# A graph layer on one core: placing matrices built per chunk, additions set ahead of column copies, and 17 more blocks of rows copied instead of gathered

## The chip, the cores and the metric

The kernel runs on one core of a Trainium2 chip. The metric is the device time of one launch in microseconds (us), the median of several runs. The engines of the core are TensorE (PE, matrix products), VectorE (DVE), ScalarE (ACT), GpSimd (POOL) and SyncE (SP); each runs its own instructions in order.

## The reference

A graph of 12,500 nodes (128 numbers each) has 412,500 edges, sorted by destination. Every edge takes the features of its source node, weighs them by a small network of its own eight scalars and by its four attributes, and the results are summed at the destination. The output is a layer norm of the input plus a mix.

```python
f0 = x0 @ W1_0e / sqrt(32); f1 = einsum('nui,uw->nwi', x1, W1_1o) / sqrt(32)   # features of nodes
e0, e1 = feat0[edge_src], feat1[edge_src]                  # gathered for every edge
h = gelu(gelu(edge_scalar_attr @ W_mlp1 / sqrt(8)) @ W_mlp2 / 8)
w00, w01, w10, w11 = h @ Wp_00, h @ Wp_01, h @ Wp_10, h @ Wp_11
out0_a = w00 * e0 * ea0;  out0_b = w11 * sum(e1 * ea1, -1) / sqrt(3)
out1_a = (w01 * e0) * ea1;  out1_b = w10 * e1 * ea0
n0, n1 = segment_sum(concat(out*_a, out*_b), edge_dst) / sqrt(32) / sqrt(2)
y = c * self(x) + s * (n0 @ W2_0e, n1 @ W2_1o) / 8
out = layernorm(x + y)
```

## The kernel before

Edges are worked on in **runs** of 512 (four blocks of 128 edges, one edge per partition), 806 in all; four runs make a **chunk** (CH = 4), 202 in all. The loop goes over runs `s`, with `c, k = divmod(s, CH)`, so k is a run's place in its chunk. The order of instructions on PE, ACT, DVE and SP is the order in which this loop writes them; nothing moves them.

**Rows for the edges.** A table of features (one row of 128 numbers per node) lies in HBM. `gather(s)` issues one indirect DMA on POOL for each block of 128 edges of run s (L197), 19 runs ahead of its use, into one of 20 buffers G. Some blocks come another way:

- The *picked* blocks: the transposed input xT lies in SBUF, one column per node. `pick_nodes` loads up to 32 column addresses into registers of an engine by one register load (L154, TENSOR_LOAD), and `pick` then copies that many columns, one instruction each, into a tile gt (L165 on DVE, L167 on ACT). After 128 columns, `picked_rows` multiplies gt by the weights on PE (L173) and ACT writes the block into G (L174). `COLS` says over how many runs 128 columns are spread: 5 on DVE (24 or 28 columns in each run) and 6 on ACT. DVE picks one block in 5 runs, ACT one in 6.
- One block of every 14th run comes by 128 row DMAs from SP (`aid`).
- The first 18 runs gather raw input rows, and PE makes the features.

**One run on DVE.** `messages(s)` makes three products of weights and G (L574, then L577 twice). `placing(s)` compares a row of numbers with one column to make a 0/1 matrix PL (L600). Then come the register load (L154) and the column copies of the run (L165).

**One chunk.** PE sums the messages of a run into windows (`segments`, L591), and at k = 1 of the next chunk `place(c - 1)` multiplies by PL (L607). At k = 2 `add(c - 1)` loads four addresses (L611) and adds four results into the running sums (L616); each addition waits for the one before it. At k = 3 `select(c + 1)` builds the 0/1 matrices of the next chunk by three operations (L559, L566, L567, of which L566 waits for L559). About every eighth chunk, `norm` (L636 to L668) finishes 512 nodes at k = 3, and `clear_sums` (L371) clears the next tile of sums in four pieces. The order at the end of a run is this:

```python
messages(s); placing(s); pick_nodes(DVE, s); pick(DVE, P)
if k == 2: add(c - 1)
if k == 3: norm(...)
elif clearing: clear_sums(...)
if k == 3: select(c + 1)
```

Of the kernel before, what the change touches and what calls it, by code (L numbers as in the profile page):

```python
# [8 lines left out]
F32 = mybir.dt.float32  # L9
# [3 lines left out]
OP = mybir.AluOpType  # L13
PE = mybir.EngineType.PE
ACT = mybir.EngineType.Activation
DVE = mybir.EngineType.DVE
# [4 lines left out]
P = 128  # L21
# [4 lines left out]
SB = P * Q  # L26
J = 8
W = 32
CH = 4
# [13 lines left out]
AID_FROM = 36  # L43
AID_LEAD = 16
STEPS = 12
COLS = {DVE: 5, ACT: 6}
COL_Q = {DVE: Q - 2, ACT: Q - 3}
COL_TURN = {DVE: (8, 0), ACT: (16, 1)}
LNB = 2
# [3 lines left out]
def gnn_kernel(ctx: ExitStack, tc: tile.TileContext, x, src, dst, ea4, ea8, w1_0, w1_1, wm1, wm2,  # L53
# [8 lines left out]
    nc = tc.nc  # L62
# [43 lines left out]

    picked = {}
    for e, per in COLS.items():
        picked[e], (t, k) = [], COL_TURN[e]
        while True:  # L110
            at = t + per + 1
            at += (k - at) % CH
            if at + 2 >= NS - 1:
                break
            picked[e].append((t, at, at + 2))
            t += per
    pick_of = {(e, s): i for e, g in picked.items() for i, (_, _, s) in enumerate(g)}
    assert AID_FROM >= raw_runs and AID_LEAD < LEAD and P % ROWS == 0 and STEPS <= AID
    assert all(raw_runs <= g[0][2] and 0 < len(g) <= 2 * P for g in picked.values())
# [5 lines left out]
    def aid_load():  # L125


        nc.sync.dma_start(aid_at, sub(src, AID_FROM * SB + (Q - 1) * P, [[AID * SB, len(aided)], [1, P]]))
        nc.vector.tensor_scalar(aid_at, aid_at, float(4 * P), None, op0=OP.mult)
        for e, g in picked.items():  # L130
            cycle = CH // math.gcd(CH, COLS[e])
            for h in range(0, len(g), P):
                part = g[h:h + P]
                rows = cst.tile([len(part), P], I32, name=f"pick{len(pick_rows)}")
                for i in range(min(cycle, len(part))):
                    n = len(part[i::cycle])
                    nc.sync.dma_start(rows[i::cycle], sub(src, part[i][2] * SB + COL_Q[e] * P,
                                                          [[cycle * COLS[e] * SB, n], [1, P]]))
                nc.vector.tensor_scalar(rows, rows, 4.0, float(x_at), op0=OP.mult, op1=OP.add)
                for i in range(len(part)):  # L140
                    pick_rows[e, h + i] = rows[i:i + 1]
# [2 lines left out]

    def pick_nodes(e, s):

        per = COLS[e]
        i, t = divmod(s - COL_TURN[e][0], per)
        if not 0 <= i < len(picked[e]):
            return  # L150
        if t == 0:
            GT[e, i] = wk.tile([P, P], F32, name=f"gt{list(picked).index(e)}", bufs=3)
        r0, r1 = (n * (P // 4) // per * 4 for n in (t, t + 1))
        _, r = nc.values_load_multi_w_load_instructions(  # L154
            pick_rows[e, i][:, r0:r1], engines=[e], min_val=x_at, max_val=x_at + 4 * (N - 1),
            skip_runtime_bounds_check_because="addresses of columns")
        for k in range(r1 - r0):
            at = r[k].with_bounds(guaranteed_mod_val=0, out_of_modulus=4)
            picking[e].append((GT[e, i][:, r0 + k:r0 + k + 1], x_bytes[:, bass.ds(at, 4)].bitcast(F32)))
# [433 lines left out]
        if r % 2 or s == NS - 1:  # L593
            nc.scalar.activation(SG[c][:, r // 2 * 2:r + 1, :], SEG[c][:, r // 2 * 2:r + 1, :], AF.Copy)  # L594

    def placing(s):

        b, r = divmod(s, P)
        PL[s] = wk.tile([P, P], F32, name="pl", bufs=CH + 1)
        nc.vector.tensor_scalar(PL[s], iota, colv[b][:, r:r + 1], None, op0=OP.is_equal)  # L600

    def place(c):
        ns = min(CH, NS - c * CH)
        ST[c] = pt = ps.tile([P, CH, 4, W], F32, name="m", bufs=1)
        for k in range(ns):
            s = c * CH + k
            nc.tensor.matmul(pt[:, k].rearrange("p a n -> p (a n)"), SG[c][:, k, :], PL[s], start=True, stop=True)  # L607

    def add(c):
        ns = min(CH, NS - c * CH)  # L610
# [189 lines left out]
    with tc.manual_schedule(engines={PE, ACT, DVE, SP}):  # L800
        load_raw_rows(nc.sync, 0, min(2, raw_runs))
        load_w1(nc.scalar)
        if raw_runs > 2:
            load_raw_rows(nc.scalar, 2, raw_runs)
        for s in range(min(LEAD - 2, raw_runs)):
            gather(s)
        nc.vector.tensor_scalar(ident, diag, 0.0, None, op0=OP.is_equal)
        for b in range(min(3, NG)):
            XT[b] = load_nodes(b)
        make_wf()  # L810
        clear()
        loads = list(weight_loads())
        extra = {2: lambda: load_edges(0), 3: lambda: load_attributes(0), NG // 2 - 2: lambda: turn_attributes(0), 4: lambda: load_raws(0), NG // 2: lambda: load_indices(0),
                 NG // 2 + 3: make_w1b, NG // 2 + 5: make_ws, NG - 6: lambda: radial(0), NG - 4: lambda: mlp1(0),
                 NG - 2: lambda: mlp2(0), NG - 1: make_wpost}
        for b in range(NG + 2):
            if b < NG:
                turn(b)
            if 0 < b <= NG:
                features_of(b - 1)  # L820
            if 1 < b:
                store_nodes(nc.scalar, table, b - 2, PF[b - 2])
            if b + 3 < NG:
                XT[b + 3] = load_nodes(b + 3)
            if b > 4 and loads:
                nc.sync.dma_start(*loads.pop(0))
            if b in extra:
                extra[b]()
        assert not loads
        for c in range(1, min(EDGES_AHEAD, NCH)):  # L830
            load_edges(c)
        if aided:
            aid_load()
        for s in range(min(LEAD - 2, raw_runs), min(LEAD - 1, NS)):
            gather(s)
        if NCH > 1:
            radial(1)
            mlp1(1)
            mlp2(1)
        weights(0)  # L840
        select(0)
        turn_rows(0)
        features(0)
        find_first()
        new_sums()
        nc.vector.memset(A["next"], 0.0)
        A["now"] = A["next"]
        new_sums()
        clearing = [(0, a) for a in range(4)]
        pick_nodes(ACT, 0)  # L850
        for s in range(NCH * CH + CH):
            c, k = divmod(s, CH)
            if s + LEAD - 1 < NS:
                gather(s + LEAD - 1)
            if k == 3 and c + EDGES_AHEAD < NCH:
                load_edges(c + EDGES_AHEAD)
            if s % P == P // 2 - 16 and (s // P + 1) * P < NS:
                load_raws(s // P + 1)
            if s % P == P // 2 and (s // P + 1) * P < NS:
                load_indices(s // P + 1)  # L860
            if s % ET == 8 and s - 8 + ET < NS:
                load_attributes(s // ET + 1)
            for t in range(P // ROWS):
                a = s + AID_LEAD - t * STEPS // (P // ROWS)
                if a in aided:
                    aid(a, t)
            end = c == NCH - 1
            if k % 2 == 0:
                pick(ACT, len(picking[ACT]) // 2)
            if k % 2 == 0 and s + 2 < NS:  # L870
                weights(s + 2)
            if 0 < s <= NS:
                segments(s - 1)
            if k == 0 and c + 2 < NCH:
                radial(c + 2)
            if k == (0 if end else 1) and 0 < c <= NCH:
                place(c - 1)
            if s % ET == 21 and s - 21 + ET < NS:
                turn_attributes(s // ET + 1)
            for e in picked:  # L880
                if (e, s + 2) in pick_of:
                    picked_rows(e, pick_of[e, s + 2])
            if k > 1 and c + 2 < NCH:
                pick(ACT, P)
                (mlp1 if k == 2 else mlp2)(c + 2)
                if k == 3 and c + 3 == NCH:
                    nc.scalar.activation(spent, ones, AF.Sqrt)
            pick(ACT, P)
            pick_nodes(ACT, s + 1)
            if s + 1 < raw_runs:  # L890
                turn_rows(s + 1)
            if s < NS:
                messages(s)
                placing(s)
                pick_nodes(DVE, s)
                pick(DVE, P)
            if s + 1 < raw_runs:
                features(s + 1)
            if k == (1 if end else 2) and 0 < c <= NCH:
                add(c - 1)  # L900
            if k == (1 if end else 3) and 0 < c <= NCH:
                norm(due.get(c - 1, []), last=c == NCH)
                clearing += [(c, a) for a in range(4)] if c - 1 in due and c < NCH else []
            elif clearing:
                clear_sums(clearing.pop(0)[1])
            if k == 3 and c + 1 < NCH:
                select(c + 1)
            if s == NS - 8:
                count_odd()

# [30 lines left out]
```

## Time and profile before

| | |
|---|---|
| median of 3 runs | 3655.97 us (3654.6 to 3658.94) |
| profiled execution | 3654.6 us, span of its instructions 3652.8 us |
| busy: PE, DVE, ACT, POOL | 72%, 84%, 65%, 75% |
| gathers on POOL | 2880 (72 of them from the raw input) |
| column copies on DVE, on ACT | 20,224 and 16,640 |
| register loads for them on DVE | 790 |

The profile lists groups of instructions by line, with busy time, the mean duration of one and the idle time of the engine just before them. A duration runs from the start to the end of an instruction; on DVE and ACT the next one starts before that end, so what an instruction costs in a row of work is the distance between starts. Register loads run on the engine's sequencer, which hands out the engine's instructions; the profile does not count them as busy, and marks them with a q (DVEq).

### The profile page before, as it was taken

To read this page: it belongs to the slowest core of one execution; us is meant where nothing else is said; L and a number is where in the kernel's file an instruction comes from. 1 tells how busy PE (TensorE), PEld (TensorE's weight loads), DVE (VectorE), ACT (ScalarE), POOL (GpSimd) and SP (SyncE) were. 2 spreads that over 40 slices of the span, in tenths; PEclk is the share of its full clock that TensorE was granted. 3 is DMA by queue.
4 is the path that set the end of the run, shared out by engine and by line. 5 is a ranking of instruction groups with operands and counts; after the bars stand their busy time and mean duration, and the time that the engine had idled before them with its cause. 6 is when DMAs were issued, how large, how long until landed. Compare 5 with 4: busy or idle time off the path is not lost.

```text
span 3652.8 us, 129429 instructions
## 1 busy us (share of the span) xinstructions
PE 2618.5 (72%) x29857; PEld 1938.9 (53%) x29857; DVE 3077.8 (84%) x25457; ACT 2391.7 (65%) x18614; POOL 2736.6 (75%) x2887
## 2 busy tenths in 40 slices
PE   5777777877677777677777677677677677677676
PEld 5555555655455555455555455555455555455554
DVE  3688898898898888887887888888888798798886
ACT  2377677677677667666766667666666676676673
POOL 7767777777777777777777777777777777777775
PEclk8989898788888878887788787887887787788877
DMA  9222332333332333322323322223222233233222
GB/s 207 57 57 67 63 63 64 63 63 71 63 63 65 63 63 70 63 62 63 63 59 68 67 60 63 67 60 69 64 62 63 63 63 63 65 63 62 59 64 48
DMA packets 578767, 243.66 MB, mean 67 GB/s; under 512 B 482186, under 2 KB 527072, under 8 KB 577984
## 3 DMA queue, kind: packets, MB, share of 16 engines
q0 software_dynamic: 92160, 188.93, 20.4%
q1 hardware_dynamic: 464542, 39.90, 8.9%
q10 hardware_dynamic: 21282, 6.47, 0.8%
q8 instruction: 238, 3.90, 0.5%
q14 instruction: 545, 4.46, 0.4%
HBM read 222.26 MB, written 12.80 MB: 64 GB/s over the span
## 4 chain that ended last, share of the span: by engine, by line
DVE 31%; issue 16%; POOL 16%; PE 10%; DMA 9%; SPq 7%; ACT 7%; DVEq 4%; ACTq 0%; POOLq 0%
POOL G L197 16%; DVE gt L165 13%; DMA G<-table,idx 8%; DVE M L577 7%; SPq L184 5%; ACT gt L167 3%; DVEq L154 3%; DVE M L574 3%; DVE acc L616 2%; DVE pl L600 2%; PE h L636 2%; PE seg L591 2%; PE w L532 2%; SPq L180 2%; DVE S L567 1%
## 5 line engine op out<-in xcount | busy, mean ns | idle before, releaser
L197 POOL DMA_INDIRECT G<-table,idx x2808 | 2667.1, 950 | 867.8 <-issue 737.2
L167 ACT ACTIVATE gt<-xT 128x1 f32 x16640 | 1664.4, 191 | 146.5 <-issue 144.9
L165 DVE COPY gt<-xT 128x1 f32 x20224 | 1301.6, 145 | 205.0 <-issue 194.2
L532 PE MATMUL w<-wpb,h 64*128 64x128 f32 x6448 | 730.9, 332 | 336.3 <-DVE M L577 334.0
L591 PE MATMUL seg<-M,S 128*32 128x128 f32 x12896 | 652.0, 322 | 419.1 <-DVE M L577 278.5
L532 PEld LDWEIGHTS w<-wpb,h 64*128 64x128 f32 x6448 | 587.5, 226 | 503.9 <-DVE M L577 388.9
L577 DVE TENSOR_TENSOR M<-w,G 128x384 f32<-128x384 f32 x1576 | 797.5, 548 | 0.0
L591 PEld LDWEIGHTS seg<-M,S 128*32 128x32 f32 x12896 | 343.6, 123 | 607.6 <-issue 152.1
L594 ACT ACTIVATE sg<-seg 128x256 f32<-128x256 f32 x403 | 150.9, 374 | 404.0 <-PE seg L591 391.5
L574 DVE TENSOR_TENSOR M<-w,G 128x256 f32<-128x256 f32 x788 | 323.4, 410 | 107.9 <-DMA G<-table,idx 93.7
L515 PE MATMUL h<-h,w2b 64*64 64x256 f32 x3232 | 319.2, 413 | 90.2 <-ACT h L504 87.4
L607 PE MATMUL m<-pl,sg 128*128 128x128 f32 x1612 | 333.0, 370 | 1.5 <-DVE acc L616 0.8
L607 PEld LDWEIGHTS m<-pl,sg 128*128 128x128 f32 x1612 | 282.1, 264 | 59.7 <-issue 57.6
L174 ACT ACTIVATE G<-h 128x128 f32<-128x128 f32 x288 | 79.3, 275 | 331.0 <-PE h L173 293.7
L500 PE MATMUL h<-eT,w1b 64*128 64x128 f32 x3232 | 280.3, 322 | 5.8 <-ACT eT L493 5.8
L500 PEld LDWEIGHTS h<-eT,w1b 64*128 64x128 f32 x3232 | 237.8, 222 | 56.1 <-issue 45.5
L515 PEld LDWEIGHTS h<-h,w2b 64*64 64x64 f32 x3232 | 146.6, 139 | 216.9 <-ACT h L504 177.4
L616 DVE TENSOR_TENSOR acc<-m,acc 128x128 f32 x806 | 234.2, 291 | 30.8 <-issue 2.7
L600 DVE TENSOR_SCALAR pl<-iota,colv 128x128 f32<-128x128 f32 x806 | 241.2, 299 | 5.1 <-PE m L607 5.1
L504 ACT ACTIVATE h<-h 128x512 f32<-128x512 f32 x404 | 215.7, 585 | 35.3 <-PE h L500 33.8
L520 ACT ACTIVATE h<-h 128x512 f32<-128x512 f32 x404 | 214.1, 580 | 19.8 <-PE h L515 14.0
L173 PE MATMUL h<-wf,gt 128*128 128x128 f32 x576 | 146.0, 345 | 14.4 <-ACT eT L493 10.2
(117 smaller groups left out, 1489.8 us busy)
## 6 DMA issues: line engine op xcount, KB each, us to landing
G<-table SPq DMA_DIRECT2D x7040, 0.5 KB
G<-table,idx POOLq DMA_INDIRECT x2808
e<-in_edge_attr SPq DMA_DIRECT2D x201, 64.0 KB
xt<-in_x SPq DMA_DIRECT2D x24, 256.0 KB
table<-ft ACTq DMA_DIRECT2D x24, 256.0 KB
xt<-in_edge_attr SPq DMA_DIRECT2D x24, 256.0 KB
out<-y SPq DMA_DIRECT2D x24, 256.0 KB
xt<-in_dst SPq DMA_DIRECT2D x5, 256.0 KB
```

The costliest lines, as they stand in the source:

```text
L165: nc.vector.tensor_copy(to, col)
L167: nc.scalar.activation(to, col, AF.Copy)
L197: nc.gpsimd.indirect_dma_start(out=G[s][:, q, :], out_offset=None, in_=x if s < raw_runs else table, in_offset=bass.IndirectOffsetOnAxis(a ...
L500: nc.tensor.matmul(p1[h][:, j // 2, j % 2, :], w1b[rows, j, :], eT[c][rows, :], start=True, stop=True)
L515: nc.tensor.matmul(p2[r][k * HID:(k + 1) * HID, h * n:(h + 1) * n], w2b[rows, :], H1[c][h][rows, k * n:(k + 1) * n], start=True, stop=True)
L532: nc.tensor.matmul(WP[i][:, q, :], H2[c][q % 2][rows, k, q // 2, :], wpb[rows, :], start=True, stop=True)
L574: nc.vector.tensor_tensor(m[:, :, :, :MUL], w[:, :, :2 * MUL].rearrange("p q (a u) -> p q a u", a=2), g[:, :, None, :MUL].to_broadcast([P, ...
L577: nc.vector.tensor_tensor(m[:, :, j, MUL:].rearrange("p q (i u) -> p q i u", i=3), w[:, :, None, (2 + j) * MUL:(3 + j) * MUL].to_broadcast ...
L591: nc.tensor.matmul(SEG[c][q * W:(q + 1) * W, r, :], own[:, r * Q + q, col:col + W], M[s][:, q, h, :], start=h == 0, stop=h == 1)
L600: nc.vector.tensor_scalar(PL[s], iota, colv[b][:, r:r + 1], None, op0=OP.is_equal)
L607: nc.tensor.matmul(pt[:, k].rearrange("p a n -> p (a n)"), SG[c][:, k, :], PL[s], start=True, stop=True)
L616: nc.vector.tensor_tensor(a, ST[c][:, k], a, op=OP.add)
```

## The change

Three things change.

- Picks on DVE are spread over 4.5 runs instead of 5: blocks of 4 and of 5 runs take turns, with 32 columns in each run of the first kind and 24 or 28 of the second. There are 175 picked blocks in place of 158, and 2863 gathers in place of 2880.
- `placing` is called once a chunk, at k = 0, and makes the four matrices by one operation on 128 x 512, with two buffers in place of five small ones.
- The register load and the column copies of a run come last in the run: behind the additions, the norm and the selection. Clearing is done at k = 1 alone.

```diff
-COLS = {DVE: 5, ACT: 6}
+COLS = {DVE: 4.5, ACT: 6}
...
-            at = t + per + 1
+            t, z = (t0 + int(n * per) for n in (len(picked[e]), len(picked[e]) + 1))
+            at = z + 1
             at += (k - at) % CH
...
-            picked[e].append((t, at, at + 2))
-            t += per
+            picked[e].append((range(t, z), at, at + 2))
...
-            cycle = CH // math.gcd(CH, COLS[e])
+            cycle = next(n for n in range(1, P) if n * COLS[e] % CH == 0)
...
-    def placing(s):
-        b, r = divmod(s, P)
-        PL[s] = wk.tile([P, P], F32, name="pl", bufs=CH + 1)
-        nc.vector.tensor_scalar(PL[s], iota, colv[b][:, r:r + 1], None, op0=OP.is_equal)
+    def placing(c):
+        n = min(CH, NS - c * CH)
+        b, r = divmod(c * CH, P)
+        PL[c] = wk.tile([P, CH, P], F32, name="pl")
+        nc.vector.tensor_tensor(PL[c][:, :n], iota[:, None, :].to_broadcast([P, n, P]),
+                                colv[b][:, r:r + n, None].to_broadcast([P, n, P]), op=OP.is_equal)
...
                 messages(s)
-                placing(s)
-                pick_nodes(DVE, s)
-                pick(DVE, P)
+                if k == 0:
+                    placing(c)
...
             if k == (1 if end else 2) and 0 < c <= NCH:
                 add(c - 1)
             if k == (1 if end else 3) and 0 < c <= NCH:
                 norm(due.get(c - 1, []), last=c == NCH)
...
-            elif clearing:
+            elif k == 1 and clearing:
                 clear_sums(clearing.pop(0)[1])
             if k == 3 and c + 1 < NCH:
                 select(c + 1)
+            if s < NS:
+                pick_nodes(DVE, s)
+                pick(DVE, P)
```

More of the change, by code (lines that the diff above doesn't have):

```diff
@@ L108, in gnn_kernel @@
     for e, per in COLS.items():
-        picked[e], (t, k) = [], COL_TURN[e]
+        picked[e], (t0, k) = [], COL_TURN[e]
         while True:
-            at = t + per + 1
+            t, z = (t0 + int(n * per) for n in (len(picked[e]), len(picked[e]) + 1))
+            at = z + 1
             at += (k - at) % CH
@@ L114, in gnn_kernel @@
                 break
-            picked[e].append((t, at, at + 2))
-            t += per
+            picked[e].append((range(t, z), at, at + 2))
+    step_of = {(e, s): (i, s - g[i][0][0]) for e, g in picked.items() for i in range(len(g)) for s in g[i][0]}
     pick_of = {(e, s): i for e, g in picked.items() for i, (_, _, s) in enumerate(g)}
@@ L137, in aid_load @@
                     nc.sync.dma_start(rows[i::cycle], sub(src, part[i][2] * SB + COL_Q[e] * P,
-                                                          [[cycle * COLS[e] * SB, n], [1, P]]))
+                                                          [[int(cycle * COLS[e]) * SB, n], [1, P]]))
                 nc.vector.tensor_scalar(rows, rows, 4.0, float(x_at), op0=OP.mult, op1=OP.add)
@@ L145, in pick_nodes @@
     def pick_nodes(e, s):
-        per = COLS[e]
-        i, t = divmod(s - COL_TURN[e][0], per)
-        if not 0 <= i < len(picked[e]):
+        if (e, s) not in step_of:
             return
+        i, t = step_of[e, s]
+        per = len(picked[e][i][0])
         if t == 0:
@@ L606, in place @@
             s = c * CH + k
-            nc.tensor.matmul(pt[:, k].rearrange("p a n -> p (a n)"), SG[c][:, k, :], PL[s], start=True, stop=True)
+            nc.tensor.matmul(pt[:, k].rearrange("p a n -> p (a n)"), SG[c][:, k, :], PL[c][:, k, :], start=True, stop=True)
     def add(c):
```

## The prediction

> **What bounds the kernel now.** I read the page first, for POOL's gathers and DVE's copies and placing matrices.
>
> ```profile
> span 3652.8 us, 129429 instructions
> L197 POOL DMA_INDIRECT G<-table,idx x2808 | 2667.1, 950 | 867.8 <-issue 737.2
> L165 DVE COPY gt<-xT 128x1 f32 x20224 | 1301.6, 145 | 205.0 <-issue 194.2
> L600 DVE TENSOR_SCALAR pl<-iota,colv 128x128 f32<-128x128 f32 x806 | 241.2, 299 | 5.1 <-PE m L607 5.1
> ```
>
> POOL's gaps are "issue", 0.3 us behind each gather: gathers follow each other every 1.25 us without a stop. DVE has 194.2 us of "issue" ahead of copies. Which of the two engines sets the end? I located the messages of each run (L574). Run 20 starts at 205.2 us, run 40 at 280.6, run 260 at 1202.1, run 796 at 3593.1. Next, DVE's waits in two stretches: runs 40 to 260, then run 260 to 3610.0 us.
>
> ```profile
> DVE gt L165 <- issue: 38.0, 89, 1.7
> DVE bst L645 <- ACT y L641: 24.7, 6, 5.0
> ...
> DVE gt L165 <- issue: 149.9, 324, 1.7
> DVE M L574 <- DMA G<-table,idx: 84.3, 68, 3.0
> DVE bst L645 <- ACT y L641: 50.9, 16, 6.0
> ```
>
> In the first stretch no message waits for a gather: POOL is ahead, DVE goes at its own rate, (1202.1 - 280.6) / 55 = 16.75 us a chunk. In the second, messages wait for gathers: 2407.9 / 135 = 17.84 us a chunk, POOL's rate. So DVE has about 1.1 us a chunk to spare. The question is whether the change costs DVE more than that.
>
> The decisive row is the register load. DVE's timeline in one stretch, with the chain of waits through it:
>
> ```profile
> 1015.46 0.28 DVE L600 TENSOR_SCALAR pl<-iota,colv 128x128 f32<-128x128 f32 x1
> 1015.65 1.54 DVE L165 COPY gt<-xT 128x1 f32 x24
> 1018.56 1.54 DVE L165 COPY gt<-xT 128x1 f32 x24
> 1020.02 1.26 DVE L616 TENSOR_TENSOR acc<-m,acc 128x128 f32 x4
> 1021.20 0.41 DVE L574 TENSOR_TENSOR M<-w,G 128x256 f32<-128x256 f32 x1
> 1022.46 0.28 DVE L600 TENSOR_SCALAR pl<-iota,colv 128x128 f32<-128x128 f32 x1
> 1023.25 0.15 DVE L165 COPY gt<-xT 128x1 f32 x1 [0.52 <-issue]
> ...
> 1020.99 0.04 DVE acc L616
> 1021.02 0.05 issue
> 1021.07 0.05 DVEq L574
> ```
>
> The loads' own rows, two single ones:
>
> ```profile
> L154 DVEq TENSOR_LOAD <-pick x1: 1612/1612/1612, 1016.8 to 1016.8; - x1
> L154 DVEq TENSOR_LOAD <-pick x1: 1858/1858/1858, 1021.3 to 1021.3; - x1
> ```
>
> The first (24 columns) starts at 1016.8, before the copies of the previous run are done: the sequencer runs ahead, and messages and placing hide the load. The second (28) stands behind additions. Each addition waits for the one before; only when the fourth has started (1020.99) does the sequencer go on, and the load starts at 1021.30. It ends at 1023.16, the copies start 0.09 later, and DVE has stood idle 0.52 us even though three messages and a placing lay between.
>
> **The change, part by part (us a chunk, DVE at its own rate, from 16.75).**
>
> *Stalls before, removed:* 38.0 / 55 = 0.69.
>
> *Length of the new loads.* 24 columns take about 1.64 us and 28 about 1.90 over the whole trace (1.61 and 1.86 in the rows above), 0.064 per column; 32 columns then take 2.16 (estimate). By the loop, 261 loads have 24, 174 have 28 and 352 have 32: 1.93 on average. Copies start 0.09 behind.
>
> *k = 2.* The load now stands directly behind the additions. It starts 0.01 after the fourth, which takes 0.21 to the next start. Idle: 1.93 + 0.09 + 0.01 - 0.21 = 1.82.
>
> *k = 3.* The load stands behind the selection. L566 waits for L559, so the load starts with L566; L566 and L567 cover 0.21 + 0.47 (from start to start) = 0.68. Idle: 1.93 + 0.09 + 0.02 - 0.68 = 1.36.
>
> *k = 1.* Only three messages, 0.33 + 2 x 0.46 = 1.26, lie ahead of the load, and a clearing (0.40) in about half of the chunks. Loads in clear stretches start some 0.35 ahead of the messages. 1.93 + 0.09 - 0.35 - 1.26 = 0.41, without clearing; with it nearly nothing. Loads at k = 1 stalled 0.14 more than this reasoning gives, so I take 0.35, between 0.1 and 0.6.
>
> *k = 0.* Messages and the large placing cover 1.86: 0.08, at most 0.3.
>
> Together 3.61, so 2.92 more than before.
>
> *Copies.* 17 blocks x 128 = 2176 more, 11.4 a chunk. From start to start (1.54 - 0.145) / 23 = 0.061: +0.69.
>
> *Placing.* Four by 0.19 (1015.46 to 1015.65) are 0.76, with 0.03 of waits 0.79. The trace has no comparison of 128 x 512. The nearest rows are L566 (128 elements, 0.21) and L567 (384, 0.47): 0.13 per 128, so 0.60. Bounds 0.47 and 0.79. Taken: -0.19. [...]
>
> *Norm.* About every eighth chunk, DVE waits some 4 us for ACT (24.7 / 6). The copies of k = 2 and their stall now lie between the additions and that wait, which shortens it by about 1.4: -0.18 (0 to -0.35). PE and ACT keep their places.
>
> *Gathers.* 17 fewer x 1.25 = 21 us less on POOL, 17.73 a chunk; worth that only if POOL is still last. The 17 more products on PE and evictions on ACT (0.3 us each) lie beside other work.
>
> *Start.* Eight more loads of column addresses on SP, some 0.65 each, lie ahead of the loop, whose first messages start at 107.8: 0 to 5 us. In the raw runs DVE waits for ACT anyway. I take +2, at most +9.
>
> The sum is 16.75 + 2.92 + 0.69 - 0.19 - 0.18 = 19.99, above POOL's 17.73: DVE becomes the bound from the start, and POOL will run 20 buffers ahead. Behind each stalled load stand the copies, then the next run's messages, for which PE's sums and POOL's free buffers wait.
>
> Total: 205.2 + 2 up to run 20; 776 runs = 194 chunks x 19.99 = 3878; from run 796 to the end 59.7 before, about 50 now, since no gather holds the last runs back: 4135 for the span. The profiled execution was 1.8 above its span and 1.4 below the median: **4137 us**, slower by 13%. The terms' bounds are worth about ±0.4 a chunk: 4055 to 4215.
>
> **Rivals.**
>
> *A, gathers still set the pace (faster).* The sequencer gets past instructions that wait, and the loads start under messages as now. Then DVE needs 16.75 + 0.69 - 0.19 = 17.25, POOL's 17.73 rules, and the time is 3656 - 21 = 3635. It decides if new stalls stay under 17.73 - 17.25 = 0.48 a chunk. For it: loads with nothing waiting ahead of them start early. Against it: the second load above, and the register operations ahead of the additions, which the trace has only some 0.01 after the start of the preceding addition. [...]
>
> *B, half of it.* Only the load behind the additions is exposed; behind the selection it starts early, and 1.36 becomes about 0.3. 18.93 x 194 + 257 + 3 = 3932. Against it: L566 waits for L559 as an addition waits for its predecessor.
>
> *C, more.* Emptied by the stalls, the sequencer loses its lead at k = 0 and k = 1 as well, and loads start 0.1 after the messages, as behind additions now: about 0.45 more at each, 0.9 a chunk, 4310. For it: late in the run some loads do start so. Against it: 24 or more copies of 0.061 give the sequencer time to catch up.
>
> **How the numbers follow.** Forecast 0.77, A 0.04, B 0.07, C 0.12. A range from 4010 to 4230 takes in the forecast's own bounds and reaches toward B and C; A, most of B and half of C lie outside. No change means within 0.2% (7 us), about what a measurement of this kernel can tell. Faster comes from A alone, 0.04; same 0.01, where stalls just reach the break-even; slower 0.95.
>
> **What would show it.** "Issue" ahead of the copies should rise from 194 us to about 700, mostly in pieces of about 1.8 us behind the additions and 1.4 us behind the selection; DVE's busy time should rise by about 100 us, its share fall; messages should no longer wait for gathers; POOL should wait for messages. Loads starting ahead of the additions or the selection would prove me wrong, as would a chunk under 18 us.

## The result, and the profile after

The changed kernel takes 4111.97 us (median of 4 runs, 4103.59 to 4114.89) beside 3655.28 us for the kernel before (4 runs): a ratio of 1.1247, 95% interval 1.1224 to 1.127. The profiled execution took 4103.59 us, its span 4101.8 us.

The page of the changed kernel: span, engines, and the groups of gathers, column copies and the first message of a run (busy, mean ns | idle before, and what ended it):

```profile
span 4101.8 us, 131172 instructions
PE 2854.1 (70%) x29891; PEld 2112.8 (52%) x29891; DVE 3148.9 (77%) x27026; ACT 2412.9 (59%) x18631; POOL 2752.2 (67%) x2870
L198 POOL DMA_INDIRECT G<-table,idx x2791 | 2681.8, 961 | 1233.6 <-issue 781.2
L166 DVE COPY gt<-xT 128x1 f32 x22400 | 1430.9, 144 | 666.8 <-issue 655.7
L575 DVE TENSOR_TENSOR M<-w,G 128x256 f32<-128x256 f32 x788 | 326.7, 415 | 0.6 <-ACT G L175 0.2
```

The first message of a run in the kernel before, and POOL's waits for messages before and now (us in total, times, longest):

```profile
L574 DVE TENSOR_TENSOR M<-w,G 128x256 f32<-128x256 f32 x788 | 323.4, 410 | 107.9 <-DMA G<-table,idx 93.7
```

```profile
POOL G L197 <- DVE M L577: 37.9, 123, 0.7
POOL G L198 <- DVE M L578: 353.0, 163, 14.1
```

The bound has moved. Idle time ahead of the copies rose from 205 to 667 us, nearly all of it "issue". Messages waited 108 us before, mostly for gathers, and now 0.6. POOL, which had paused 868 us in its own steps of 0.3, now pauses 1234, 353 of them for messages. Every engine's busy share fell, DVE's from 84% to 77%: the engine that sets the end is less busy than before, because it stands idle between its own instructions.

VectorE's timeline through one chunk, k = 2 and 3, then 0 and 1 of the next:

```profile
2023.56 1.26 DVE L619 TENSOR_TENSOR acc<-m,acc 128x128 f32 x4
2027.01 2.03 DVE L166 COPY gt<-xT 128x1 f32 x32 [2.19 <-issue]
...
2030.74 0.55 DVE L568 TENSOR_TENSOR S<-oh,e 128x384 f32<-128x384 f32 x1
2032.80 2.27 DVE L166 COPY gt<-xT 128x1 f32 x32 [1.50 <-issue]
...
2036.24 0.68 DVE L602 TENSOR_TENSOR pl<-iota,colv 128x512 f32<-128x512 f32 x1
2036.94 2.03 DVE L166 COPY gt<-xT 128x1 f32 x32
...
2040.29 0.48 DVE L372 MEMSET acc<- 128x512 f32 x1
2040.97 2.04 DVE L166 COPY gt<-xT 128x1 f32 x32 [0.20 <-issue]
```

Idle time stands above all where the load follows a waiting instruction: 2.19 us behind the additions, 1.50 behind the selection, none behind the large placing, 0.20 behind a clearing. The chain of waits through the first of these places (start, length, what):

```profile
2024.53 0.29 DVE acc L619
2024.82 2.10 DVEq L155
2026.92 0.09 issue
2027.01 1.46 DVE gt L166 x22
```

The row of the load at this place (duration min/median/max in ns, then when it starts):

```profile
L155 DVEq TENSOR_LOAD <-pick x1: 2382/2382/2382, 2024.5 to 2024.5; - x1
```

The load starts at 2024.5, with the fourth addition, and the chain runs through it: 2.10 us in which DVE has nothing to do. Copies start 0.09 after its end. It is the same at every such place from run 40 to 790: the 187 loads at k = 2 start a median 0.014 us after the fourth addition, the 187 at k = 3 a median 0.016 us after L567, the operation of the selection that waits for L560, and none starts before it.

### The profile page after: what moved, and what is told of

It is laid out like the page before. It is cut to its first block, busy times and chain, and to the rows that moved or that the text cites. A ratio compares the mean times of both kernels' runs of the same rounds, so it can differ in the third digit from the quotient of the medians.

```text
span 4101.8 us, 131172 instructions
## 1 busy us (share of the span) xinstructions
PE 2854.1 (70%) x29891; PEld 2112.8 (52%) x29891; DVE 3148.9 (77%) x27026; ACT 2412.9 (59%) x18631; POOL 2752.2 (67%) x2870
## 3 DMA queue, kind: packets, MB, share of 16 engines
q0 software_dynamic: 91616, 187.81, 17.9%
## 4 chain that ended last, share of the span: by engine, by line
DVE 29%; issue 6%; SPq 6%; DVEq 5%; PE 4%; ACT 2%; DMA 1%; POOL 1%; ACTq 0%; POOLq 0%
DVE gt L166 14%; DVE M L578 7%; DVEq L155 5%; SPq L185 5%; DVE M L575 2%; DVE acc L619 2%; PE h L639 1%; SPq L181 1%; DVE pl L602 1%; ACT gt L168 1%; POOL G L198 1%; DVE S L567 1%; DMA G<-table,idx 1%; PE seg L592 0%; DVE acc L372 0%
## 5 line engine op out<-in xcount | busy, mean ns | idle before, releaser
L166 DVE COPY gt<-xT 128x1 f32 x22400 | 1430.9, 144 | 666.8 <-issue 655.7
L533 PE MATMUL w<-wpb,h 64*128 64x128 f32 x6448 | 831.0, 360 | 466.2 <-DVE M L578 462.7
L592 PE MATMUL seg<-M,S 128*32 128x128 f32 x12896 | 691.6, 342 | 499.7 <-DVE M L578 385.6
L533 PEld LDWEIGHTS w<-wpb,h 64*128 64x128 f32 x6448 | 666.2, 249 | 653.0 <-DVE M L578 530.1
L592 PEld LDWEIGHTS seg<-M,S 128*32 128x32 f32 x12896 | 363.7, 129 | 700.1 <-issue 295.5
L516 PE MATMUL h<-h,w2b 64*64 64x256 f32 x3232 | 333.7, 421 | 93.9 <-ACT h L505 91.2
L610 PE MATMUL m<-pl,sg 128*128 128x128 f32 x1612 | 374.7, 405 | 1.3 <-ACT sg L595 1.3
L610 PEld LDWEIGHTS m<-pl,sg 128*128 128x128 f32 x1612 | 319.0, 294 | 68.9 <-issue 67.0
L516 PEld LDWEIGHTS h<-h,w2b 64*64 64x64 f32 x3232 | 148.4, 140 | 229.1 <-ACT h L505 192.5
L619 DVE TENSOR_TENSOR acc<-m,acc 128x128 f32 x806 | 233.6, 290 | 23.6 <-PE m L610 2.1
L174 PE MATMUL h<-wf,gt 128*128 128x128 f32 x610 | 171.7, 378 | 7.6 <-DVE bst L648 7.6
L174 PEld LDWEIGHTS h<-wf,gt 128*128 128x128 f32 x610 | 155.8, 310 | 10.8 <-issue 10.8
```

The costliest lines, as they stand in the source:

```text
L166: nc.vector.tensor_copy(to, col)
L174: nc.tensor.matmul(pt, GT.pop((e, i)), wf, start=True, stop=True)
L516: nc.tensor.matmul(p2[r][k * HID:(k + 1) * HID, h * n:(h + 1) * n], w2b[rows, :], H1[c][h][rows, k * n:(k + 1) * n], start=True, stop=True)
L533: nc.tensor.matmul(WP[i][:, q, :], H2[c][q % 2][rows, k, q // 2, :], wpb[rows, :], start=True, stop=True)
L592: nc.tensor.matmul(SEG[c][q * W:(q + 1) * W, r, :], own[:, r * Q + q, col:col + W], M[s][:, q, h, :], start=h == 0, stop=h == 1)
L619: nc.vector.tensor_tensor(a, ST[c][:, k], a, op=OP.add)
```

## Experiments

Two theories were set against each other. Theory 1: the register load lost the work that covered it, because the sequencer doesn't get past an instruction that waits. Theory 2: the place or the number of the copies, not the load, costs the time.

Of twelve runs, eight fell on two other chips, on which the kernel before itself takes 5681 and 5585 us. Four are told first, from chips where it takes about 3655 us.

**All but the order** (e6): the changed kernel with load and copies put back behind the messages.

```diff
                 messages(s)
                 if k == 0:
                     placing(c)
+                pick_nodes(DVE, s)
+                pick(DVE, P)
...
-            elif k == 1 and clearing:
+            elif clearing:
...
-            if s < NS:
-                pick_nodes(DVE, s)
-                pick(DVE, P)
```

> The changed kernel with the order of before: load and copies directly behind the messages and the placing. Theory 1: loads of 1.93 us stand behind messages alone in three runs of four; idle 0.05 at k = 0, 0.6 at k = 1, 0.46 at k = 2, 0.72 at k = 3; 18.3 us a chunk, about 3820 us. The order's share of the change is then some 290 us, the rest comes from the longer loads, the lost cover and the copies. Theory 2 (order free): 4112 us.

Measured: 3713.03 us, ratio to the kernel before 1.0155 (1.014 to 1.0171). So putting the order back takes 4112 - 3713 = 399 of the 457 us away, and theory 2's "order free" falls. (What the order would cost the kernel before by itself was forecast at 300 us; e1 and e1b tried it, both on the other two chips.) From the page:

```profile
L166 DVE COPY gt<-xT 128x1 f32 x22400 | 1433.5, 144 | 301.4 <-issue 292.2
L575 DVE TENSOR_TENSOR M<-w,G 128x256 f32<-128x256 f32 x788 | 320.7, 407 | 0.8 <-issue 0.4
```

As many copies, 301 us of idle time ahead of them in place of 667, and still no message that waits for a gather: DVE remains the bound. On average (runs 40 to 790) the idle time ahead of a run's copies was, by k, 0.04, 0.31, 0.36 and 0.78 us, in place of 0.08, 0.20, 1.82 and 1.27 in the changed kernel. My 3820 was too high: idle time came to 1.49 us a chunk, not the 1.83 of the forecast, above all at k = 1 (0.31, not 0.6). That is 66 of the 107 us.

**Half of each load** (e5c), everything else as changed. Each address loaded serves two columns, so half of the picked rows are those of another node:

```diff
-            pick_rows[e, i][:, r0:r1], engines=[e], ...
+            pick_rows[e, i][:, r0:(r0 + r1) // 2 if e == DVE else r1], engines=[e], ...
...
-            at = r[k].with_bounds(...)
+            at = r[k // 2 if e == DVE else k].with_bounds(...)
```

> The same kernel as in e5_half_load (half of the addresses are loaded, each column is copied twice; copies, gathers and order as in the changed kernel). Idle ahead of the copies on two other chips was 0.94 us at k = 2, 0.44 at k = 3 and none at k = 0 and 1, as theory 1 has it. On a chip on which the kernel before takes about 3656 us, theory 1 gives 19.8 - 3.4 + 1.4 = 17.8 us a chunk, about 3720 us; theory 2 (place or number of the copies costs) 4112 us.

Measured: 3723.25 us, ratio 1.0192 (1.0175 to 1.0209), 17.9 us a chunk. All its loads in one row (ns), then its timeline at two such places:

```profile
L155 DVEq TENSOR_LOAD <-pick x787: 845/1123/2108, 150.7 to 3667.2; - x197
```

```profile
2001.48 1.26 DVE L619 TENSOR_TENSOR acc<-m,acc 128x128 f32 x4
2003.92 2.03 DVE L166 COPY gt<-xT 128x1 f32 x32 [1.19 <-issue]
...
2007.65 0.55 DVE L568 TENSOR_TENSOR S<-oh,e 128x384 f32<-128x384 f32 x1
2008.82 2.03 DVE L166 COPY gt<-xT 128x1 f32 x32 [0.62 <-issue]
```

With a load of half the length, 32 copies in the same late place wait 1.19 and 0.62 us in place of 2.19 and 1.50. The averages by k are 0.00, 0.00, 0.99 and 0.44. Place and number of the copies are those of the changed kernel, and 389 of the 457 us are gone. This is the purest test of the cause, and theory 1 had its time within 0.1%, with the idle times read from two earlier runs of the same kernel (e5 and e5b below).

**The placing alone** (e2): the kernel before with one operation of 128 x 512 a chunk.

```diff
                 messages(s)
-                placing(s)
+                if k == 0:
+                    placing(c)
                 pick_nodes(DVE, s)
                 pick(DVE, P)
```

> The kernel before with one placing operation of 128 x 512 a chunk alone. Theory 1: the operation itself costs 0.19 us a chunk less, but three of four runs lose 0.19 us of cover for their load, and idle time ahead of the copies rises by about 0.4 us a chunk; DVE needs about 17.0 us where it runs at its own rate (runs 40 to 260; 16.75 before), still under the gathers' 17.84, so the time stays within 0.3%. Theory 2 (fewer, larger operations are a gain for DVE): the same total, but 16.55 us a chunk in runs 40 to 260.

Measured: 3673.5 us, ratio 1.0044 (1.0029 to 1.006): slower, while I had expected 0.3% at most. The cover went as expected in part: idle ahead of copies rose at k = 2 and 3, which lost their placing, from 0.16 and 0.45 to 0.31 and 0.61 us, and fell from 0.11 to 0.01 at k = 0. At k = 1, which lost it too, it stayed at 0.30. Together 0.2 us a chunk were lost, not 0.4. Runs 40 to 260 took 16.82 us a chunk, only 0.07 more than before; the loss of time came later, where gathers set the pace: 18.03 us a chunk in place of 17.84. The gathers themselves grew longer. The page's group of gathers, then one gather in POOL's timeline, and the placing beside it in VectorE's:

```profile
L197 POOL DMA_INDIRECT G<-table,idx x2808 | 2697.1, 960 | 863.4 <-issue 727.0
```

```profile
602.79 1.45 POOL L197 DMA_INDIRECT G<-table,idx  x1 [0.30 <-issue]
```

```profile
602.75 0.68 DVE L601 TENSOR_TENSOR pl<-iota,colv 128x512 f32<-128x512 f32 x1
```

Gathers have 960 ns on average in place of 950, 30 us more in all. This one began 0.04 us after a placing and took 1.45 us; the median is 0.945. Gathers that overlap a placing averaged 1.05 us, those that don't 0.951.

**Spread of 4.75 runs** (e7): the kernel before, `COLS = {DVE: 4.75, ACT: 6}`.

> The kernel before with blocks spread over 4.75 runs (order and placing as before): 8 gathers fewer. Theory 1: copies add 0.33 us a chunk and longer loads 0.35, so DVE needs 17.4 us a chunk, still under the gathers' 17.79; the gathers still set the pace and the time falls by about 10 us, to 3645. If DVE and POOL do not overlap that well near the balance: 3655 to 3680.

Measured: 3657.72 us, ratio 1.0007 (0.9998 to 1.0016): no change. From run 20 to 796 a chunk took 17.41 us in place of 17.46, 11 us in all, but the first messages started at 121.2 us in place of 107.8. DVE's waits show why (the last line is that of the kernel before):

```profile
DVE gt L166 <- issue: 208.3, 440, 1.8
DVE pick L140 <- DMA pick<-in_src: 16.3, 4, 10.1
```

```profile
DVE pick L139 <- DMA pick<-in_src: 0.8, 1, 0.8
```

DVE waits 16.3 us for the column addresses, which this spread fetches by 32 small loads ahead of the loop; 0.8 us in the kernel before, with 8. What the fewer gathers gave, the start took; in both kernels the last gather ends 22 us before the end, so gathers still set it. So I tried a spread of 4.8, with 10 such loads (e8).

> The kernel before with blocks spread over 4.8 runs (6 gathers fewer; the addresses come by 10 loads ahead of the loop, 8 in the kernel before and 32 with a spread of 4.75, where the first messages started 13 us later). Theory 1: start as before, DVE about 17.3 us a chunk, so the gathers still end last: 7.5 us less, about 3648 us. If DVE's own rate decides here: 3655 to 3670.

It fell on a chip on which the kernel before takes 5585 us: 5607.2 us, ratio 1.0042 (1.0022 to 1.0062). Whether it beats the kernel before elsewhere stays open. On the chips at 3655 us no version did; on the two others the kernel of e4, told next, was 3% faster than the kernel before; it was not run on the faster chips.

**On the two other chips.** There the kernel before takes some 27 us a chunk (an estimate from its time), and something other than these loads holds it back, so times say little; nor was the changed kernel itself run there. But the idle time can still be read in the profiles. Ahead of copies it is given here for the first copy of a run alone: between the copies of a run these chips show another 2.7 to 5.6 us a chunk (0.03 in the kernel before at 3655 us), whose cause is open.

The order alone, run twice (e1: 5652.77 us, ratio 0.9965, 0.994 to 0.9989; e1b: 5576.41 us, 0.9997, 0.9977 to 1.0016):

```diff
                 messages(s)
                 placing(s)
-                pick_nodes(DVE, s)
-                pick(DVE, P)
...
                 select(c + 1)
+            if s < NS:
+                pick_nodes(DVE, s)
+                pick(DVE, P)
```

> The kernel before with the order of the change alone: register load and copies last in the run, clearing at k = 1; blocks spread over 5 runs and placing per run as before. Theory 1 (loads lose their cover): loads of 24 and 28 columns last 1.75 us on average; idle ahead of the copies about 0.07 at k = 0, 0.15 at k = 1, 1.64 at k = 2, 1.08 at k = 3, 2.94 a chunk in place of 0.75, so 19.0 us a chunk and about 3955 us. Theory 2 (the order is free, the time went to more copies and longer loads): within 0.5% of the kernel before, since the copies are as many as before.

> The same kernel as in e1_order_alone, on a chip on which the kernel before takes about 3656 us. Theory 1 (loads lose their cover): idle ahead of the copies 0.07, 0.15, 1.64 and 1.08 us at k = 0 to 3, 19.0 us a chunk, about 3955 us. Theory 2 (the order is free): within 0.5% of the kernel before.

Idle by k averaged 0.14 to 0.15, 0.93 to 0.96, 1.65 and 1.10 us: at k = 2 and 3 what theory 1 had, 1.64 and 1.08, but at k = 0 and 1 more than its 0.07 and 0.15. Why the time didn't move isn't shown: no profile of the kernel before from these chips exists. In time, these runs decide nothing.

The load put back, copies last (e4: 5496.21 us, ratio 0.9691, 0.9652 to 0.973; e4b: 5438.08 us, 0.9734, 0.9706 to 0.9761):

```diff
                 if k == 0:
                     placing(c)
+                pick_nodes(DVE, s)
...
             if s < NS:
-                pick_nodes(DVE, s)
                 pick(DVE, P)
```

> The changed kernel with the register load put back directly behind the messages and the placing, the copies still last. Theory 1: the load is covered by the messages again; about 0.07 us idle at k = 0, 0.36 at k = 1, 0.94 at k = 2 (now ahead of the additions, whose address load queues behind) and 0.37 at k = 3; 18.3 us a chunk, about 3805 us. The idle time should move from ahead of the copies to ahead of the additions and of the selection. Theory 2 (it is the copies' late place that costs): unchanged, 4112 us.

> The same kernel as in e4_load_ahead, on a chip on which the kernel before takes about 3656 us. Theory 1: idle time moves from ahead of the copies to ahead of the additions (0.94 us a chunk, the address load waits behind the long load) and of the selection (0.4); nearly none is left ahead of the copies at k = 2 and 3; about 18.2 us a chunk, 3790 to 3810 us. Theory 2 (the late place of the copies costs): unchanged, 4112 us.

Idle ahead of the first copy is 0.00 at k = 2 and 3; it now stands ahead of the additions, 0.99 us, and of the selection, 0.36 to 0.38, where theory 1 had 0.94 and 0.37 to 0.4. The second agrees: such idle time ends a median 0.09 us after the end of a register load, and in e1 and e5 there is none ahead of the selection. The first agrees in part by luck: some two thirds of the 0.99 end within 0.35 us of a load's end, and the rest has other causes, since in e5 and e5b, with the load behind the additions, 0.35 to 0.40 stand there too. So the idle time follows the load, not the copies. VectorE's timeline of e4b, the same two places:

```profile
2030.54 1.27 DVE L619 TENSOR_TENSOR acc<-m,acc 128x128 f32 x4 [0.60 <-PE h L501]
2031.73 1.66 DVE L166 COPY gt<-xT 128x1 f32 x24
...
2035.42 0.55 DVE L568 TENSOR_TENSOR S<-oh,e 128x384 f32<-128x384 f32 x1
2035.89 1.54 DVE L166 COPY gt<-xT 128x1 f32 x24
```

Copies follow additions and selection without a gap.

Half of each load, the same kernel as e5c (e5: 5516.95 us, ratio 0.9718, 0.9682 to 0.9753; e5b: 5447.94 us, 0.9746, 0.972 to 0.9772):

> The changed kernel, but DVE loads only half of the addresses and copies each column twice (so half of the picked rows are those of another node). Copies, gathers and order stay. Theory 1: loads of 12 to 16 columns last about 1.0 us, so 0.95 idle at k = 2, 0.45 at k = 3, none at k = 0 and 1; about 17.9 us a chunk, close to the gathers' 17.73: about 3740 us. Theory 2 (the place or the number of the copies costs): unchanged, about 4112 us.

> The same kernel as in e5_half_load (half of the addresses are loaded, each column is copied twice), on a chip on which the kernel before takes about 3656 us. Theory 1: loads of about 1.0 us, idle about 0.95 at k = 2 and 0.4 at k = 3, none at k = 0 and 1; 17.8 to 17.9 us a chunk, 3720 to 3740 us. Theory 2 (place or number of the copies): about 4112 us.

Idle ahead of the first copy 0.00, 0.01, 0.99 and 0.42 us in both, as in e5c. More copies alone (e3: 5717.72 us, ratio 1.0065, 1.0039 to 1.0091), the kernel before with a spread of 4.5:

> The kernel before with blocks spread over 4.5 runs alone (order and placing as before). Theory 1: copies add 0.69 us a chunk, and loads of up to 32 columns outlast the messages and the placing by 0.73 us a chunk more than before, so DVE needs about 18.2 us a chunk, more than the gathers' 17.73: about 3790 us, slower by 3 to 4%. Theory 2 (more copies cost what the change lost): the same place, but most of the 12%: above 3950 us. If gathers alone set the pace: 3635 us.

Idle ahead of the first copy 0.25, 0.90, 0.24 and 0.63 us, together 2.02 a chunk, where theory 1 had 1.48 (0.73 more than the 0.75 that e1's expectation gives for the kernel before). Much of it stands at k = 1, as in e1 on the same chip. In time, inconclusive.

## Why the prediction was right, step by step

- **The bound.** That DVE had only some 1.1 us a chunk to spare, and that it would become the bound, held: messages no longer waited for gathers, and POOL waited for messages. The signs came as named: 656 us of "issue" ahead of the copies (about 700 forecast), 71 us more busy time on DVE (about 100).
- **The stalls**, a chunk, runs 40 to 790, as forecast and measured: k = 0, 0.08 and 0.08; k = 1, 0.35 and 0.20; k = 2, 1.82 and 1.82; k = 3, 1.36 and 1.27. Together 3.61 and 3.37. At k = 1 I had carried over 0.14 of an unexplained excess, which wasn't there: loads at k = 1 started a median 0.16 us ahead of the messages in the kernel before, and 0.32 now. Loads of 32 columns took 2.15 us; 2.16 had been estimated.
- **Rival A** fell at L619: a waiting addition held the sequencer back, and the load with it. None of the 187 loads at k = 2 started before the fourth addition. Where nothing waited, loads started early, with up to 10 of the instructions ahead of them not yet started (9 for 105 of the 790 loads of the kernel before, 10 for one).
- **Rivals B and C.** At k = 3 loads started with L567 (L566 of the kernel before), as forecast, and 1.27 us of idle time stood there, not B's 0.3. At k = 0 and 1 loads kept a lead of 0.29 and 0.32 us (median) over the messages, which C had lost.
- **Copies.** 1430.9 - 1301.6 = 129 us more busy time; 2176 x 0.061 = 133 had been forecast.
- **Placing.** The large one took 0.60 from its start to the next (median), as taken from L566 and L567, and the four small ones 4 x 0.193 = 0.77, as taken from L600. But the term was too small, as the sum below shows: a small placing ahead of a stall had cost its whole 0.28, not 0.19.
- **The norm** was wrong in sign. I had 0.18 us a chunk less waiting, and there was more:

```profile
DVE bst L648 <- ACT y L644: 113.4, 24, 8.0
```

The row before was this:

```profile
DVE bst L645 <- ACT y L641: 78.3, 23, 6.0
```

That is 0.17 a chunk more over the whole trace. I took the additions for what starts the norm's products on PE. But in both kernels PE starts them a median 5.4 us before that wait ends, right behind the products of the edge network of k = 3 (L515 before, L516 now), while the last addition now ends 9.3 us before it on average, in place of 6.9. With placing and copies gone from between the messages and the wait, DVE just arrives earlier (a median 1.2 us after PE's start, 2.4 before) and waits longer.
- **Start.** +2 forecast; run 0 starts 4.6 us later and run 20 7.5 (at 212.7 us). DVE waited 8.2 us for the column addresses, 0.8 in the kernel before.
- **Sum.** 19.99 us a chunk forecast, (4053.5 - 212.7) / 194 = 19.80 measured; from run 796 to the end 48.3 us, 50 forecast. 4137 forecast (its last step adds up to 4138), 4112 measured. That it came so close is in part luck, for the errors of the terms cancel. By distances from start to start, this is what a chunk took in the kernel before (runs 40 to 260) and in the changed one (runs 40 to 790):

| us a chunk | before | changed | difference | forecast |
|---|---|---|---|---|
| idle ahead of copies | 0.76 | 3.38 | +2.62 | +2.92 |
| copies | 6.30 | 6.93 | +0.63 | +0.69 |
| placing | 1.04 | 0.64 | -0.40 | -0.19 |
| wait of the norm | 0.55 | 0.64 | +0.09 | -0.18 |
| messages, additions, selection | 7.08 | 7.34 | +0.26 | 0 |
| all | 16.75 | 19.84 | +3.09 | +3.24 |

The rows left out changed by -0.11. The forecast had nothing for the fifth row: where a stall follows, the operation ahead of it takes its whole length (an addition 0.29 us, not the 0.21 to the next start).

## What to carry to other kernels

A register load held the engine's sequencer the longer the more it loaded (24, 28 and 32 addresses took 1.64, 1.90 and 2.15 us; in e5c 12 and 16 took 0.87 and 1.13, but 14 took 1.36, which stays unexplained). In these runs it was hidden only where the engine had queued work that waited for nothing (0.08 us idle behind the messages and the large placing). Behind a chain of instructions that wait for each other it was almost fully exposed (1.82 us idle behind the additions); so place it directly behind the longest stretch without waits, here the messages, and count what covers it before that cover is merged or moved. A small operation that looks like a cost (here the placing) can be the cover: without it, e2's idle time ahead of the copies rose by 0.15 us at k = 2 and by 0.16 at k = 3.

## What the runs showed of the hardware beyond that

- Gathers of GpSimd that started while certain operations of VectorE ran took longer than the median of 0.944 us. In the changed kernel the 153 that started within the placing of 128 x 512 took 1.16 us on average and up to 1.50 (in e2 up to 1.48); in the kernel before the 84 within L567 took 1.09, those within L566 1.01 and within L559 0.97. These four operations have two inputs in SBUF. Within the placing of the kernel before, with one tensor input, gathers took 0.96, and within the messages, which have one input in PSUM, 0.944. No run varied the inputs alone, so it isn't shown that they are the cause.
- The granted clock of TensorE fell from 0.83 to 0.76, while PE was busy for 70% of the span in place of 72%. No cost of it can be seen here: the one long wait of DVE that runs through PE is the norm's, and from PE's start on it to the end of that wait the median is 5.4 us in both kernels.
- On the two slower chips operations of VectorE, ScalarE and GpSimd last as long as elsewhere: in e1, from 2000 to 2030 us, a copy on DVE took 0.15 us and 15 of 17 gathers 0.94 (one 0.95, one 1.24), and 24 copies on ACT in its chain took 2.33, beside 0.145, a median of 0.944 and at least 2.32 in the kernel before. Products of PE took longer: the five longest stretches of 16 products L515 in e1's chain took 2.46 to 3.26 us, the three longest in that of the kernel before 1.85 to 2.52, at a granted clock of 0.64 in place of 0.83. And single copies on DVE without any wait between them start some 0.7 us apart in places (in e1 at 2000.15, 2000.85 and 2001.58 us). What holds them apart there wasn't settled.
